# One explicit order for all five engines of a two-layer graph-attention kernel, with operand splits and products issued in two steps

## The chip, the cores and the metric

The kernel runs on one core of a Trainium2 chip. The metric is the device time of one execution in microseconds (us). A statement such as "2055.66 us" is the median of several executions. A ratio is the mean time of one kernel's fast runs over the mean of the other's fast runs in the same rounds, with a 95% interval, so it is not quite the ratio of the medians quoted beside it. A difference under 2% counts as "same".

## The reference, cut to what matters

The input x has 128 batches of 128 tokens by 512 features; adj is one 128x128 matrix used for all batches.

```python
# layer 0: graph convolution, maximum, residual, layer norm
A = einsum('od,bdn->bon', adj, x);  C = A + b
out0 = max(relu(A[:, :, None, :] + (C - A)[:, :, :, None]), axis=-1)
x = layernorm(x + out0)
# layer 1: masked attention with 8 heads, projection, inner norm, residual, layer norm
q, k, v = split(x @ w_qkv)                        # 512 -> 3 * 512
attn = softmax(where(adj == 0, -inf, q @ k.T * scale))
o = (attn @ v) @ w_proj + b_proj
x = layernorm(x + o + (layernorm(o) * gamma + beta))
```

Per batch this is one convolution, eight score and eight attention products with 64 wide heads, and 512-deep products for q, k, v and the projection. The deep products dominate.

## The kernel before

Batches go in 32 groups of four. Precision comes from splitting an operand a into a high part h, a rest l and a third form d, so that one product becomes 12 matmuls of 128x512: four of h, four of l, four of d. In the names of the trace, `x_h x_l x_d` are the split input, `oh ol od` the split attention output (for the last eight batches it lies in the buffers of `w_h w_l w_d`), `po` (as `pp_('o', 48)`) a projection, `pp_(13, 2)` a product of group 13, `psc` scores, `eT` the transposed attention weights, `pa` a convolution, `xb` the residual.

```python
def split(key, src, dsts):
    fh, fl, fd = dsts
    xh = work.tile([P, KC, P], FP, tag="xh", name=f"xh_{key}")
    nc.vector.tensor_scalar(xh.bitcast(I32), src.bitcast(I32), HIGH, None, op0=ALU.bitwise_and)
    hs[key] = fh, xh                               # ScalarE casts xh to fh later: split_high
    nc.vector.tensor_tensor(fl, src, xh, op=ALU.subtract)
    nc.vector.scalar_tensor_tensor(fd, fl.bitcast(FP), -HALF, xh, op0=ALU.mult, op1=ALU.add)

def product(key, two, terms):
    # ... pm, pd: two PSUM banks
    for kc in range(KC):
        h, l, _ = terms(kc)
        nc.tensor.matmul(pm, *h, start=(kc == 0), stop=False)
        nc.tensor.matmul(pm, *l, start=False, stop=(kc == KC - 1))
    for kc in range(KC):
        nc.tensor.matmul(pd, *terms(kc)[2], start=(kc == 0), stop=(kc == KC - 1))
```

The program is written as a plan: each call has a place in us, and the plan is sorted by place. TensorE and ScalarE are pinned to the order of the plan; VectorE, GpSimd and the queue of transfers (SyncE) get their order from a scheduler.

```python
plan.sort(key=lambda p: p[:2])
run([p for p in plan if p[0] < 0], None)
run([p for p in plan if p[0] >= 0], {mybir.EngineType.PE, mybir.EngineType.Activation})
```

Of the kernel before, what the change touches and what calls it, by code (L numbers as in the profile page):

```python
# [10 lines left out]
I32 = mybir.dt.int32  # L11
AF = mybir.ActivationFunctionType
# [12 lines left out]
def tile_adj_resnorm_d2(  # L25
# [37 lines left out]
    nc = tc.nc  # L63
# [19 lines left out]
    xs, x1s, rms, pa, mv0s, pts, hs = {}, {}, {}, {}, {}, {}, {}  # L83
# [101 lines left out]
    def add_0(b):  # L185
        g, i = divmod(b, G)
        if i == 0:
            mv0s[g] = small.tile([P, G, 3], FP, tag="sum0", bufs=2, name=f"sum0_{g}")
        nc.scalar.activation(
            xs[b], xs[b], AF.Identity, bias=rms[g][:, i : i + 1], accum_out=mv0s[g][:, i, 0:1],  # L190
        )
# [35 lines left out]
    def split(key, src, dsts):  # L227

        fh, fl, fd = dsts
        xh = work.tile([P, KC, P], FP, tag="xh", name=f"xh_{key}")  # L230
        nc.vector.tensor_scalar(xh.bitcast(I32), src.bitcast(I32), HIGH, None, op0=ALU.bitwise_and)  # L231
        hs[key] = fh, xh
        nc.vector.tensor_tensor(fl, src, xh, op=ALU.subtract)  # L233
        nc.vector.scalar_tensor_tensor(  # L234
            fd, fl.bitcast(FP), -HALF, xh, op0=ALU.mult, op1=ALU.add,
        )
# [5 lines left out]
    def split_high(key):  # L242
        nc.scalar.copy(*hs.pop(key))


    def product(key, two, terms):
# [7 lines left out]
        for kc in range(KC):  # L254
            h, l, _ = terms(kc)
            nc.tensor.matmul(pm, *h, start=(kc == 0), stop=False)
            nc.tensor.matmul(pm, *l, start=False, stop=(kc == KC - 1))
        for kc in range(KC):
            nc.tensor.matmul(pd, *terms(kc)[2], start=(kc == 0), stop=(kc == KC - 1))
        pps[key] = pm, pd  # L260
# [112 lines left out]
    def project(b):  # L373
        parts = [*zip(oTs.pop(b), proj_forms)]
        product(("o", b), b % 2 == 0, lambda kc: [(f[:, kc, :], w[:, kc, :]) for f, w in parts])
# [59 lines left out]
    plan = []  # L435
# [3 lines left out]


    def weights_step(b, u):
        at(u, transpose_e, b)
        at(u + 1.0, weights_T, b)
        return u + 0.9

    def x_step(b, u):
        at(u, transpose_x, b)
        at(u + 0.5, split_x, b)
        at(u + 3.0, split_high, b)
        return u + 0.45  # L450

    def scores_step(b, u):
        at(u, scores, b)
        at(u + 1.0, masked, b)
        return u + 1.0

    def attend_step(b, u, ready):
        at(u, attend, b)
        at(max(u + 1.0, ready), heads, b)
        at(max(u + 1.0, ready) + 0.8, split_high, ("o", b))  # L460
        return u + 1.0

    def conv_step(b, u):
        at(u, conv, b)
        at(u + 1.0, conv_max, b)
        return u + 0.9

    def dense_step(g, j, u, two):
        at(u, dense, g, j, two)
        at(u + 1.9, dense_main, g, j)  # L470
        at(u + 2.8, dense_rest, g, j)
        return u + 2.8

    def project_step(b, u):
        at(u - 5.0, bias, b)
        at(u, project, b)
        at(u + 1.9, projected_main, b)
        at(u + 2.8, projected_rest, b)
        return u + 2.8

    def normed(b, u, v, w, z):

        at(u - 9.0, residual, b)
        at(u - 3.0, residual_o, b)
        at(u, stats, b, 1)
        at(v, norm_1, b)
        at(w, stats, b, 2)
        at(z, norm_2, b)

    def layer_0(b, u, adds, norms):  # L490

        at(u, relu_0, b, 2)
        for i in range(2):
            at(adds + 0.9 * i, add_0, b + i)
            at(adds + 1.8 + 0.9 * i, stats_0, b + i)
        at(adds + 3.7, rstd_0, b, 2)
        for i in range(2):
            at(norms + 1.5 * i, norm_0, b + i)
            at(norms + 1.0 + 1.5 * i, keep_0, b + i)
            at(norms + 25.0 + 1.5 * i, beta_0, b + i)  # L500

    def first_pair(g, t):

        last, now, nxt = (g - 1) * G, g * G, (g + 1) * G
        u = t
        if g:
            for i in range(2):
                u = weights_step(last + i, u)
        for i in range(2):
            u = x_step(nxt + i, u)  # L510
        for i in range(2):
            at(u + 0.5, load_x, nxt + G + i) if g + 2 < NG else None
        for i in range(2):
            u = scores_step(now + i, u)

        if g:
            for i in range(2):
                u = attend_step(last + i, u, u + 1.0 + 5.3 * i)
        for i in range(2):
            u = dense_step(g, 2 + i, u, i == 1)  # L520
            if g:
                u = project_step(last + i, u)
        return u

    def second_pair(g, t):
        last, now, nxt = (g - 1) * G, g * G, (g + 1) * G
        u = t
        if g:
            for i in range(2, 4):
                u = weights_step(last + i, u)  # L530
        for i in range(2, 4):
            u = x_step(nxt + i, u)
        for i in range(2, 4):
            at(u + 0.5, load_x, nxt + G + i) if g + 2 < NG else None
        for i in range(2, 4):
            u = scores_step(now + i, u)
        if g:
            for i in range(2, 4):
                u = attend_step(last + i, u, u + 1.0 + (0.0, 7.1 if g + 2 < NG else 5.3)[i - 2])
        return u  # L540

    def dense_phase(g, t):

        last, far = (g - 2) * G, (g + 1) * G
        u = t

        def convs(i, u):
            if far < B:
                for k in range(i, i + 2):
                    u = conv_step(far + k, u)  # L550
            return u

        if g:
            u = convs(0, u)
        for n in range(2 * KC):
            if g == 0 and n in (2, 4):
                u = convs(n - 2, u)
            u = dense_step(g, G + n, u, n % 2 == 0 or n == 1 and g > 1)
            if n < 2 and g > 1:
                u = project_step(last + 2 + n, u)  # L560
            if n == 1 and g:
                u = convs(2, u)
        if g < NG - 1:
            for i in range(2):
                u = dense_step(g, i, u, i == 0)
        return u


    for b in range(G):
# [13 lines left out]
        at(u + 8.5 + 0.2 * b, split_high, b)  # L583
        at(u + 9.0, load_x, G + b)
# [6 lines left out]
    layer_0(G, 12.0, 13.0, 19.0)  # L591
    layer_0(G + 2, 19.0, 20.0, 34.0)

    t = dense_phase(0, 0.0)
    for g in range(NG - 1):
        last, far = (g - 1) * G, (g + 2) * G
        u = first_pair(g, t)
        u = second_pair(g, u)
        for i in range(G):
            at(t + (8.7, 13.5, 29.5, 34.0)[i], row_max, g * G + i)  # L600
            at(t + (10.3, 15.5, 30.5, 36.0)[i], exps, g * G + i)
            at(t + (24.0, 30.0, 42.0, 46.0)[i], weights, g * G + i)
        if g:
            normed(last, t + 22.0, t + 31.5, t + 35.5, t + 39.5)
            normed(last + 1, t + 31.0, t + 39.5, t + 43.0, t + 47.0)
            normed(last + 2, t + 45.0, t + 48.5, t + 52.0, t + 56.0)
            normed(last + 3, t + 52.0, t + 56.0, t + 60.0, t + 66.0)
        if far < B:
            for i, places in enumerate(((30.5, 39.5, 53.0), (43.0, 46.0, 66.5)) if g else ((16.0, 17.0, 24.0), (23.0, 24.0, 34.0))):
                layer_0(far + 2 * i, *(t + p for p in places))  # L610
        t = dense_phase(g + 1, u)


    g = NG - 1
    last, now = (g - 1) * G, g * G
    u = t
    def finish_step(b, u):
        at(u - 12.0, residual, b)
        at(u + 4.0, residual_o, b)
        at(u + 5.6, stats, b, 1)  # L620
        at(u + 8.5, norm_1, b)
        at(u + 12.0, stats, b, 2)
        at(u + 16.5, norm_2, b)
        return project_step(b, u)

    def finish_step(b, u):
        at(u - 12.0, residual, b)
        at(u + 4.0, residual_o, b)
        at(u + 5.6, stats, b, 1)
        at(u + 8.5, norm_1, b)  # L630
        at(u + 12.0, stats, b, 2)
        at(u + 16.5, norm_2, b)
        return project_step(b, u)

    for p in (0, 2):
        for i in (p, p + 1):
            u = weights_step(last + i, u)
        for i in (p, p + 1):
            u = scores_step(now + i, u)
        for i in (p, p + 1):  # L640
            u = attend_step(last + i, u, 0.0)
        for i in (p, p + 1):
            u = dense_step(g, i, u, i % 2 == 0)
            u = finish_step(last + i, u)
    for i in range(4):
        v = t + (6.0, 9.0, 22.0, 25.0)[i]
# [48 lines left out]
```

## Time and profile before

The time before is 2055.66 us (median of 3, 2052.22 to 2056.8). I cut the span at the first matmul of three products: (0,6), (2,6) and (31,6). The pieces are the first work, the filling of the pipeline, 29 steady groups, and the tail with its drain.

| before, us | value |
|---|---|
| span start to (0,6) | 34.86 |
| (0,6) to (2,6) | 109.76 |
| (2,6) to (31,6), 29 groups | 1815.70 |
| one undisturbed group | 62.67 |
| (31,6) to the end | 90.45 |

This is the profile of the kernel before by those stretches (the first two rows of the table are one stretch here). The columns are the stretch, its length, then busy us and instructions of TensorE, its weight loads, VectorE, ScalarE and GpSimd, granted clock, share of DMA time, and GB/s.

```profile
0.00:144.62 144.62, 128.86 (x666) 97.07 (x666) 115.04 (x182) 97.53 (x270) 37.80 (x73) 0.94 0.51 123
144.62:1960.32 1815.70, 1798.15 (x10898) 1443.23 (x10897) 1437.49 (x2318) 1295.08 (x3709) 640.31 (x1332) 1.00 0.51 118
1960.32:2050.77 90.45, 72.18 (x473) 59.27 (x471) 67.07 (x117) 56.77 (x154) 34.59 (x79) 0.93 0.33 91
```

### The profile page before, as it was taken

The numbers are of one execution on the slowest core, as the hardware profiler recorded it, in microseconds if no ns is written. First come the engines' busy times: TensorE is split into PE (matmuls) and PEld (weight loads), VectorE is DVE, ScalarE is ACT, GpSimd is POOL, SyncE is SP. The second block draws the span as 40 slices with busy tenths as digits, with TensorE's granted clock in tenths as the row PEclk, the third lists the DMA queues.
The fourth block names the chain that finished last, engine by engine and source line by source line (L and its number), as shares of the span: only waits on it lengthen the run. The fifth ranks groups of instructions, "written<-read, shape, count | busy, mean of one in ns | idle before, by whom it ended". The sixth has DMA issues, their size and how long they took to land.

```text
span 2050.8 us, 35140 instructions
## 1 busy us (share of the span) xinstructions
PE 1999.2 (97%) x12033; PEld 1599.6 (78%) x12033; DVE 1619.6 (79%) x2615; ACT 1449.4 (71%) x4130; POOL 712.7 (35%) x1484
## 2 busy tenths in 40 slices
PE   7999999999999999999999999999999999999996
PEld 4778878778787788787787877887877878778785
DVE  7797777887778877778877788777788777887777
ACT  6776777766777767777667677677776676776766
POOL 3232334333334323333333333233332333332324
PEclk8999999999999999999999999999999999999998
DMA  6445645455544556544555445564445554454623
GB/s 186 98 83 119 139 113 112 107 123 124 129 120 107 108 119 139 120 105 106 123 124 128 120 107 111 119 139 115 106 111 121 125 128 117 108 110 119 140 65 101
DMA packets 134436, 240.67 MB, mean 117 GB/s; under 512 B 14704, under 2 KB 18928, under 8 KB 134256
## 3 DMA queue, kind: packets, MB, share of 16 engines
q1 hardware_dynamic: 97680, 172.27, 26.7%
q0 software_dynamic: 36288, 66.08, 23.4%
q8 instruction: 95, 1.56, 0.3%
q14 instruction: 85, 0.70, 0.1%
q10 hardware_dynamic: 288, 0.07, 0.0%
HBM read 138.74 MB, written 100.66 MB: 117 GB/s over the span
## 4 chain that ended last, share of the span: by engine, by line
PE 82%; DVE 13%; issue 2%; ACT 1%; DMA 1%; POOL 1%; SPq 0%; POOLq 0%; DVEq 0%; ACTq 0%
PE pa L173 6%; PE ppt L339 5%; DVE e L309 4%; PE psc L302 3%; PE pav L352 3%; DVE xh L231 2%; DVE x_l L233 2%; PE ptx L223 2%; DVE x_d L234 2%; DVE ol L233 1%; DMA xb<-o 1%; ACT e L324 0%; DVE nmax L317 0%; POOL sum L409 0%; ACT square L402 0%
## 5 line engine op out<-in xcount | busy, mean ns | idle before, releaser
L324 ACT ACTIVATE e<-e,nmax 128x128 f32<-128x128 f32 x1024 | 396.3, 390 | 10.6 <-DVE nmax L317 10.3
L216 POOL DMA_DIRECT2D x<-in_L_gnn_ln_beta_dram x128 | 112.7, 991 | 443.4 <-DMA x<-xt 439.7
L409 POOL TENSOR_TENSOR sum<-sum,mhalf 128x1 f32<-128x1 f32 (+1 forms) x322 | 204.5, 635 | 26.7
L324 ACT ACTIVATION_READ_ACCUMULATOR e<-e,nmax 128x1 f32 x1024 | 193.5, 189 | 0.0
L391 POOL DMA_DIRECT2D xb<-o x124 | 113.2, 913 | 225.9 <-DVE sums L332 107.3
L402 ACT ACTIVATE square<-o,sum 128x512 bf16<-128x512 f32 x256 | 183.9, 718 | 10.4 <-DVE o L396 8.4
L183 POOL TENSOR_SCALAR rm<-rm,b_sb 128x2 f32<-128x2 f32 (+1 forms) x66 | 66.7, 1011 | 284.8 <-DVE rm L177 259.5
L333 DVE TENSOR_TENSOR e<-e,sums 128x1024 f32<-128x1024 f32 x128 | 154.2, 1223 | 2.2
L317 DVE TENSOR_REDUCE nmax<-e 128x8 f32<-128x1024 f32 x128 | 154.7, 1208 | 0.1
L309 DVE SCALAR_TENSOR_TENSOR e<-psc,mask 128x1024 f32<-128x1024 f32 x128 | 150.4, 1214 | 0.0
L343 ACT COPY eT<-ppt 128x1024 f32<-128x1024 f32 x128 | 123.4, 1015 | 35.0 <-PE ppt L339 35.0
L414 POOL TENSOR_SCALAR sum<-sum 128x1 f32<-128x1 f32 x256 | 99.7, 392 | 122.4 <-DVE o L396 122.2
L396 DVE SCALAR_TENSOR_TENSOR o<-o,sum,xb 128x512 f32<-128x512 f32 x128 | 95.5, 746 | 52.8 <-POOL sum L409 52.8
L408 POOL TENSOR_SCALAR sum<-sum 128x1 f32<-128x1 f32 (+1 forms) x322 | 64.4, 200 | 201.3 <-ACT square L402 186.2
L302 PE MATMUL psc<-qkT 64*128 64x128 f32 x2048 | 131.9, 278 | 0.8 <-ACT eT L343 0.7
L352 PE MATMUL pav<-eT,v 128*64 128x128 f32 x2048 | 127.5, 278 | 2.8 <-ACT eT L343 2.8
L302 PEld LDWEIGHTS psc<-qkT 64*128 64x128 f32 x2048 | 119.4, 188 | 11.9 <-issue 10.4
L173 PE MATMUL pa<-xt,adjT 128*128 128x512 f32 x256 | 126.2, 617 | 0.4 <-DVE adjT L102 0.4
L339 PEld LDWEIGHTS ppt<-ident,e 128*128 128x128 f32 x1024 | 115.7, 141 | 9.5 <-DVE v L291 0.8
L339 PE MATMUL ppt<-ident,e 128*128 128x128 f32 x1024 | 122.4, 272 | 0.6 <-DVE v L291 0.6
L352 PEld LDWEIGHTS pav<-eT,v 128*64 128x64 f32 x2048 | 112.0, 138 | 10.8 <-ACT eT L343 3.3
L423 DVE SCALAR_TENSOR_TENSOR o<-o,sum,gamma_sb 128x512 f32<-128x512 f32 x128 | 95.6, 747 | 31.4 <-ACT square L402 26.6
(4778 smaller groups left out, 5622.1 us busy)
## 6 DMA issues: line engine op xcount, KB each, us to landing
xt<-in_x_dram SPq DMA_DIRECT2D x128, 256.0 KB, 5.1
x<-xt SPq DMA_DIRECT2D x128, 256.0 KB, 3.6
x<-in_L_gnn_ln_beta_dram POOLq DMA_DIRECT2D x128, 256.0 KB, 7.4
xb<-x SPq DMA_DIRECT2D x128, 256.0 KB, 2.7
o<-in_L_gnn_b_proj_dram SPq DMA_DIRECT2D x128, 256.0 KB, 3.5
out_dram<-o SPq DMA_DIRECT2D x128, 256.0 KB, 2.7
xb<-o POOLq DMA_DIRECT2D x124, 256.0 KB, 3.9
wraw<-in_L_gnn_w_qkv_dram SPq DMA_DIRECT2D x12, 256.0 KB, 3.9
```

Source lines behind the costliest of these rows:

```text
L173: nc.tensor.matmul(pa[b], adjT, xs[b], start=True, stop=True)
L302: nc.tensor.matmul(psc[:, s, hp, :], qkT[hs, hp, i, :], qkT[hs, KC + hp, i, :], start=True, stop=True,)
L309: nc.vector.scalar_tensor_tensor(e, pscs.pop(b).rearrange("p s a m -> p (s a) m"), scale, mask_b, op0=ALU.mult, op1=ALU.add,)
L317: nc.vector.tensor_reduce(nmax, es[b], AX.X, ALU.max, negate=True)
L324: nc.scalar.activation(e[:, j, :], e[:, j, :], AF.Exp, bias=nmax[:, j : j + 1], accum_out=sums[:, j : j + 1],)
L333: nc.vector.tensor_tensor(e, e, sums[:, :, None].to_broadcast([P, H, P]), op=ALU.mult)
L339: nc.tensor.transpose(ppts[b][:, j, :], e[:, j, :], ident)
L343: nc.scalar.copy(eTs[b], ppts.pop(b))
L352: nc.tensor.matmul(pavs[b][s * HD : (s + 1) * HD, hp, :], v[:, h * HD : (h + 1) * HD], eT[:, s * HP + hp, :], start=True, stop=True,)
L391: nc.gpsimd.dma_start(xbs[b], os[b], accum_op=ALU.add)
L402: nc.scalar.activation(square, x, AF.Square, bias=s[:, 0:1], scale=-float(D), accum_out=s[:, 1:2],)
L409: nc.gpsimd.tensor_tensor(s, s, mhalf[:, :n], op=ALU.pow)
```

## The change

The intent is to take away the stalls that an automatic VectorE order leaves. Every engine is pinned, and each VectorE, ScalarE, GpSimd and transfer call gets a place relative to the TensorE step that it serves. The third split step (`split_d`) and the third part of a product (`product_d`) become calls of their own, so other work can stand between. TensorE's steps also get a new order: transposes of weights (T) and of inputs (x) take turns, product 5 goes ahead of product 4 and product 8 ahead of 7. Which products write to which PSUM pool changes too (`two`).

```diff
-        hs[key] = fh, xh
+        hs[key] = dsts, xh
         nc.vector.tensor_tensor(fl, src, xh, op=ALU.subtract)
+    def split_d(key):
+        (_, fl, fd), xh = hs[key]
         nc.vector.scalar_tensor_tensor(fd, fl.bitcast(FP), -HALF, xh, op0=ALU.mult, op1=ALU.add)
 ... the same for product and product_d ...
+    O = {... 'pair_order': [('T', 0), ('x', 1), ('T', 1), ('x', 0), ('S', 0), ('S', 1), ('AV', 0), ('AV', 1),
+                            ('dense', 2), ('po', 0), ('dense', 3), ('po', 1), ...],
+         'po_rest': [0.0, 0.48, 0.0, -0.81], 'x_hl': [0.9, 1.26, 0.32, 0.33], ...}
+        elif kind == "AV":
+            at(u, attend, b)
+            free = pe["po", b - 1] + 0.1 if b % 2 and b < B - 2 * G else -9.0
+            p = pe["po", b]
+            at(min(max(u + O["o_hl"][i], free), p - 0.2), heads, b)
+            at(min(max(u + O["o_high"][i], free + 0.01), p - 0.1), split_high, ("o", b))
+            at(min(max(u + O["o_d"][i], free + 1.85), p + 1.8), split_d, ("o", b))
 ... places for all other calls; the old step functions go ...
-    run([...], {mybir.EngineType.PE, mybir.EngineType.Activation})
+    run([...], {E.PE, E.Activation, E.DVE, E.Pool, E.SP})
```

## The prediction

> **What bounds the kernel now.** I read the page first, then the busy time by stretches, then the instructions of one group in order of time, engine by engine.
>
> ```profile
> span 2050.8 us, 35140 instructions
> PE 1999.2 (97%) x12033; PEld 1599.6 (78%) x12033; DVE 1619.6 (79%) x2615; ACT 1449.4 (71%) x4130; POOL 712.7 (35%) x1484
> PE 82%; DVE 13%; issue 2%; ACT 1%; DMA 1%; POOL 1%; SPq 0%; POOLq 0%; DVEq 0%; ACTq 0%
> ```
>
> TensorE is the bound, but its 97% says little about how much is left: the chain of work that ended last leaves it for VectorE for 13% of the span. The kernel handles 128 batches in 32 groups of 4, so I cut the middle of the run at the first matmul of the product (g,6) of successive groups:
>
> ```profile
> 833.99:896.66 62.67, 62.09 (x379) 49.83 (x377) 49.59 (x81) 44.83 (x130) 22.11 (x46) 1.00 0.52 119
> 896.66:959.32 62.66, 62.09 (x378) 49.81 (x377) 49.57 (x81) 44.81 (x130) 22.32 (x47) 1.00 0.50 119
> ```
>
> The columns are length, then busy us of PE, PEld, DVE, ACT and POOL, clock, DMA share, GB/s. A group takes 62.67 us, the same every time, at full clock; DMA is at half. The 0.58 us of idle PE per group understates what is lost, because a matmul's record overlaps the next one's. Starts tell more:
>
> ```profile
> 863.37 0.50 PE L256 MATMUL pm_(13, 2)_8666<-w_h,x_h 128*128 128x512 f32 x1
> ...
> 865.33 1.10 PE L259 MATMUL pd_(13, 2)_8667<-w_d,x_d 128*128 128x512 f32 x4
> 866.41 0.49 PE L256 MATMUL pp_('o', 48)_8687<-p_h,oh 128*128 128x512 f32 x1
> 867.48 0.50 PE L257 MATMUL pp_('o', 48)_8687<-p_l,ol 128*128 128x512 f32 x1 [0.58 <-DVE ol L233]
> 867.82 0.40 PE L256 MATMUL pp_('o', 48)_8687<-p_h,oh 128*128 128x512 f32 x1
> ...
> 870.15 0.40 PE L256 MATMUL pp_(13, 3)_8721<-w_h,x_h 128*128 128x512 f32 x1
> ```
>
> Undisturbed, matmuls start 0.233 us apart, so a product of 12 takes 2.80 us. This projection takes 870.15 - 866.41 = 3.74, so it loses **0.94**; its first matmul came another 0.14 late (four matmuls to 866.41 take 1.08, not 0.93), waiting for oh. That is 1.08 us a group, once a group. What holds it is in the VectorE rows of the same moment:
>
> ```profile
> 862.76 2.35 DVE L309 SCALAR_TENSOR_TENSOR e<-psc,mask 128x1024 f32<-128x1024 f32 x2
> 865.02 0.68 DVE L231 TENSOR_SCALAR xh_('o', 48)_8649<-pav 128x512 int32<-128x512 int32 x1
> 865.62 1.21 DVE L317 TENSOR_REDUCE nmax<-e 128x8 f32<-128x1024 f32 x1
> 866.75 0.68 DVE L233 TENSOR_TENSOR ol<-pav,xh_('o', 48)_8649 128x512 fp32r<-128x512 f32 x1
> ```
>
> A row maximum nobody needs yet stands between the two halves of the operand split, and both masks stand ahead of it. The last kind of loss is at the end:
>
> ```profile
> 2005.60 0.50 PE L257 MATMUL pp_('o', 122)_20237<-p_l,w_l 128*128 128x512 f32 x1 [1.29 <-DVE w_l L233]
> ...
> 2018.06 3.48 PE L352 MATMUL pav<-eT,v 128*64 128x128 f32 x32 [2.41 <-ACT eT L343]
> ...
> 2032.56 0.49 PE L256 MATMUL pp_('o', 126)_20497<-p_h,w_h 128*128 128x512 f32 x1 [1.18 <-ACT w_h L243]
> ```
>
> **What the Trainium skill says.** "Perfetto Trace Analysis", Identifying the Most-Contended Engine: matmul busy time is a bad measure of nearness to the roofline, as pipelined matmuls mislead. The trace agrees: 97% busy, yet 1.08 us per group recoverable. "TensorE: Matmul & The Clock Gate", Part 2, Step-by-step: matmuls stay in program order and only weight loads are pulled ahead. That fits the 0.94 us: nothing passed the waiting matmul. The same page, Architectural detail: ScalarE and VectorE are strict FIFO. The VectorE rows fit: ol runs behind nmax although its input had been there. "Perfetto Trace Analysis", Optimizing Tensor Performance: independent matmul groups should rotate through PSUM banks; the change alters that rotation.
>
> **The change, part by part.** No work is added or removed. The built programs have the same 5251, 2361 and 1702 rows on TensorE, VectorE and ScalarE; only order and PSUM banks differ.
>
> *Floor of a group.* 16 products x 2.80 = 44.80. From the starts in the TensorE rows: two pairs each of weight transposes (1.75), x transposes (0.97), scores (1.99), attention (1.90) and convolutions (3.51 for the two) give 13.22 + 3.51 = 16.73, and the step from attention to a product 0.10. Sum 61.63, rounding included; directly, 62.67 - 1.08 = **61.59**. I use the latter.
>
> *First half of the group.* New order: T0 x1 T1 x0 S0 S1 AV0 AV1 d2 po0. VectorE's is xh, xl of x1; xh, xl of x0; mask0; xd0, xd1; xh, ol of o0; mask1; od0; nmax0. With T0 at 0 and start-to-start durations from its rows of before (split steps 0.60, mask 1.17, row maximum 1.13): x0's input is there at 2.8, xl0 is done at 4.0, mask0 at 5.2, xd0 and xd1 at 6.3, ol at 7.5. The projection is due at 9.3. It has 1.8 us in hand where it was 1.1 late, so the stall goes: **-1.08 a group**, in the 30 groups that have it: 30 x 1.08 = 32.4 us.
>
> *Second half.* I carried the same sum on: ol of o2 done 0.9 before po2 is due, ol of o3 0.75 before po3; a convolution maximum frees the bank of product 5's second part 0.8 early. On ScalarE (a row's eight exponentials 3.1, eT copy 1.0), exponentials 1 end near 18.3, a square near 19.0, the two eT copies at 20.0 and 21.1; scores 2 and 3, which need those banks, are due at 20.4 and 21.3. That leaves only 0.1 to 0.3: the tightest place. I allow 0.1 us a group: **+3**.
>
> *Start.* Before product (0,4) starts at 25.03 us nearly the same scheduler is at work; later the first groups lose about 2.5 to first-time waits. Product (0,5) now goes first and VectorE is pinned to the weight splits. I take -1, with 3 either way.
>
> *End.* From the first transpose of the tail at 1977.12 to the last projection's end near 2038.5 there are 61.4 us; the steps sum to 8 x 0.87 + 4 x 0.99 + 8 x 0.95 + 12 x 2.80 = 52.1, so 9 are stalls. The transposes for the last batches get their weights sooner now, but a transpose still waits for its copy (0.4 to 0.6) and a projection for its split (0.6) with little between: about 4 remain. **-5**. The drain after the last matmul (about 12) keeps its chain.
>
> Sum: -32.4 + 3 - 1 - 5 = -35.4, so 2055.7 - 35.4 = **2020 us**.
>
> **The rivals.**
> 1. *A new wait in each group.* All queues are pinned, so one instruction waiting at VectorE's head delays all behind it. For: the 0.1 to 0.3 us at scores 2 and 3, and GpSimd, whose scalar statistics now stand behind DMA issues of 0.9 to 1.0 us. Against: VectorE works 50 of 62.7 us, and its slack lies in the second part of the products. At 0.5 us a group: 2032.
> 2. *VectorE's automatic order was worth something.* Its old scheduler filled gaps; a pinned order cannot. If VectorE falls behind by a microsecond at both attention pairs, the stall comes back in another place: about 2050. A wait worse than today's would need over 1 us a group: 2060 or more.
> 3. *The places remove more than I found.* With no residual stall, and a clean start and tail: 2055.7 - 32.4 - 4 - 7 = 2012. The transposes and convolutions have their own floor, so hardly below 2008.
>
> The transfers are no rival: half the DMA time is free, and loads are a group ahead.
>
> **Range and chances.** The steady part is regular to 0.02 us, so any error there counts 30 times; the plan looks tuned for just these waits, which speaks for the low half. The range 2009 to 2036 spans rival 3 to somewhat beyond rival 1. Two per cent faster means below about 2015, just under my estimate: 0.34. Slower by 2% needs rival 2 at its worst: 0.02. Within 2%: 0.64.
>
> **What would show it.** Right: groups of 61.6 to 61.8 us in the middle; no wait of the first projection on ol; product starts 2.80 apart; unchanged busy time on every engine; stalls in the tail halved. Wrong: groups above 62.0 with a wait on eT copies before scores (rival 1) or on ol, oh or a freed PSUM bank (rival 2); a first product much after 25 us; or groups below 61.4, which would mean my floor holds a hidden wait.

## The result and the profile after

The changed kernel takes 2039.85 us (2038.49 to 2040.23, 4 runs) beside 2054.43 us for the kernel before (2052.22 to 2056.8, 4 runs): ratio 0.9928, interval 0.991 to 0.9945. It is 14.6 us faster where 35.4 us were predicted, and the time is 3.85 us above the top of the predicted range. All outputs are right.

The line of busy times on the page, then the same three stretches, both of the kernel after:

```profile
PE 1995.0 (98%) x12033; PEld 1601.2 (79%) x12033; DVE 1652.2 (81%) x2615; ACT 1455.4 (71%) x4130; POOL 694.2 (34%) x1484
```

```profile
0.00:147.50 147.50, 128.69 (x665) 97.92 (x666) 116.08 (x181) 97.80 (x270) 31.83 (x70) 0.93 0.49 117
147.50:1941.84 1794.34, 1791.75 (x10898) 1444.18 (x10897) 1465.76 (x2316) 1300.65 (x3708) 626.33 (x1333) 1.00 0.52 119
1941.84:2038.45 96.61, 74.58 (x473) 59.09 (x471) 70.37 (x119) 56.98 (x156) 36.07 (x84) 0.92 0.37 99
```

The middle gained 21.36 us, but the start lost 2.88 and the tail 6.16. Two small signs matter later: VectorE's busy time rose by 32.6 us with the same 2615 instructions, and the tail's mean clock is 0.92 beside 0.93.

**The middle.** One group of the kernel after, in the same columns (the next one takes 61.86):

```profile
828.09:889.95 61.87, 61.87 (x378) 49.86 (x377) 50.60 (x81) 44.91 (x129) 21.51 (x47) 1.00 0.54 120
```

A group gained 0.80 us, from 62.67 to 61.87. The stall that the prediction named is gone. These are TensorE's instructions in order of time (start, us, engine, line, what), first around the first projection of a group, then around the fourth:

```profile
921.29 1.10 PE L269 MATMUL pd_(14, 2)_9368<-w_d,x_d 128*128 128x512 f32 x4
922.22 0.40 PE L261 MATMUL pm_('o', 52)_9397<-p_h,oh 128*128 128x512 f32 x1
922.46 0.40 PE L262 MATMUL pm_('o', 52)_9397<-p_l,ol 128*128 128x512 f32 x1
...
944.62 0.40 PE L261 MATMUL pp_(15, 4)_9658<-x_h,w_h 128*128 128x512 f32 x1
...
947.60 0.50 PE L261 MATMUL pm_('o', 55)_9679<-p_h,oh 128*128 128x512 f32 x1
947.94 0.39 PE L262 MATMUL pm_('o', 55)_9679<-p_l,ol 128*128 128x512 f32 x1
...
950.50 1.88 PE L174 MATMUL pa<-xt,adjT 128*128 128x512 f32 x4
```

Projection 52 starts 0.93 us after the last block of four, which is those four matmuls at 0.233, and its second matmul comes 0.24 later: no wait. But the product (15,4) takes 947.60 - 944.62 = 2.98 us and projection 55 takes 950.50 - 947.60 = 2.90 instead of 2.80 each. That is a new loss of 0.18 + 0.10 = 0.28 us a group, at the **fourth** projection, where none was before (the kernel before starts product (14,5) at 889.75, projection 51 at 892.54 and the convolution after it at 895.34). The list of waits for this window is empty; only the starts show it. VectorE at the same moment, kernel after:

```profile
942.81 0.68 DVE L178 TENSOR_REDUCE rm<-pa 128x1 f32<-128x512 f32 x1
943.41 0.68 DVE L391 SCALAR_TENSOR_TENSOR o<-pp_('o', 54)_9593,o 128x512 f32<-128x512 f32 x1
944.01 0.74 DVE L432 SCALAR_TENSOR_TENSOR o<-o,sum,gamma_sb 128x512 f32<-128x512 f32 x1
944.86 0.75 DVE L405 SCALAR_TENSOR_TENSOR o<-o,sum,xb 128x512 f32<-128x512 f32 x1
...
945.54 0.69 DVE L405 SCALAR_TENSOR_TENSOR o<-pp_('o', 54)_9593,o 128x512 f32<-128x512 f32 x1
...
946.15 0.69 DVE L232 TENSOR_SCALAR xh_('o', 55)_9642<-pav 128x512 int32<-128x512 int32 x1
946.87 0.69 DVE L234 TENSOR_TENSOR ol<-pav,xh_('o', 55)_9642 128x512 fp32r<-128x512 f32 x1
```

Here six steps from 942.81 to 946.87 take 4.06 us; at 0.60 each they would take 3.60. Independent neighbours start 0.60 apart, although each record lasts 0.68. A step that reads what its neighbour wrote starts later: xh to ol 0.72, the two norm lines 0.85. The excess of 0.46 us is larger than the loss of 0.28. Over the whole second half of the group, from xh of its first input (932.13) to this ol, the excess over 0.60 at such neighbours is 0.13 + 0.11 + 0.11 + 0.13 + 0.25 + 0.08 + 0.12 = 0.93 us.

The first matmul of projection 55 reads oh, ScalarE's cast of xh. Its row:

```profile
946.93 0.62 ACT L248 CAST oh<-xh_('o', 55)_9642 128x512 fp32r<-128x512 f32 x1 [0.32 <-DVE xh_('o', 55)_9642 L232]
```

ScalarE had been idle for 0.32 us, waiting for VectorE's xh, and the cast ends at 947.55, 0.05 us before the projection starts. So ScalarE passes the delay on; it doesn't make it.

**The tail.** TensorE, then VectorE, then the stretch that begins with projection 123 (its clock is the third number from the end), all of the kernel after:

```profile
1996.88 0.80 PE L261 MATMUL pm_('o', 123)_20460<-p_h,w_h 128*128 128x512 f32 x1 [4.49 <-ACT w_h L248]
1997.47 0.63 PE L262 MATMUL pm_('o', 123)_20460<-p_l,w_l 128*128 128x512 f32 x1
```

```profile
1980.73 0.75 DVE L432 SCALAR_TENSOR_TENSOR o<-o,sum,gamma_sb 128x512 f32<-128x512 f32 x1 [2.95 <-DMA xb<-o]
...
1994.34 0.69 DVE L232 TENSOR_SCALAR xh_('o', 123)_20439<-pav 128x512 int32<-128x512 int32 x1
```

```profile
1996.80:2001.50 4.70, 4.62 (x11) 3.66 (x12) 2.83 (x5) 1.22 (x4) 1.65 (x2) 0.50 0.72 183
```

Projection 123 waits 4.49 us for its split, which VectorE begins only at 1994.34. VectorE stood idle for 2.95 us at a norm (the row at 1980.73), which waits for the transfer that adds o to the residual. Then it works for 13.6 us, without a wait in its rows, on the norms, masks and weights that its order puts ahead of the split. So the late residual can account for at most 2.95 of the 4.49 us; the order accounts for the rest. The wait costs twice: afterwards matmuls start some 0.43 us apart instead of 0.233 at a granted clock of 0.50, where the stretch before the wait has 1.00. The Trainium skill, "TensorE: Matmul & The Clock Gate", Part 1, says that an idle window of about 3.4 us halves TensorE's clock; this trace agrees, with 0.50 right after 4.49 us of waiting. Other runs told of below don't fit that length: in e12 the clock is 0.50 in the 2.4 us after a wait of 2.52, and in e15 it stays 1.00 after one of 2.85.

**The start.** The stretch to (0,6) is unchanged (34.86 and 34.89 us); from (0,6) to (2,6) it grew from 109.76 to 112.61. Two parts are netted in this: (0,6) to (1,6) grew from 46.31 to 50.74, while (1,6) to (2,6), a group with the old stall, shrank from 63.45 to 61.87. The waits of the transfers' queue in the kernel after between 50 and 80 us (total, times, longest), and then its transfers between 50 and 85 us (count, size, median us from issue to landing):

```profile
SPq L90 <- DMA x<-xt: 12.2, 3, 7.1
```

```profile
x<-in_L_gnn_ln_beta_dram POOLq DMA_DIRECT2D x6, 256.0 KB, 8.3
x<-xt SPq DMA_DIRECT2D x4, 256.0 KB, 7.1
xt<-in_x_dram SPq DMA_DIRECT2D x4, 256.0 KB, 6.4
```

Loads of x (L90) wait 12.2 us in all for the stores `x<-xt` that free their buffers, and these stores take 7.1 us (median) to land. In the same stretch GpSimd issues the accumulating transfers of beta for the first group, four in one burst:

```profile
56.28 3.61 POOL L217 DMA_DIRECT2D x<-in_L_gnn_ln_beta_dram  x4
```

In the kernel before, these four go out one at a time, at 16.54, 20.36, 28.00 and 30.24 us.

### The profile page after: what moved, and what is told of

Its sections match the earlier page's. It is cut to its first block, busy times and chain, and to the rows that moved or that the text cites. A ratio compares the mean times of both kernels' runs of the same rounds, so it can differ in the third digit from the quotient of the medians.

```text
span 2038.5 us, 35386 instructions
## 1 busy us (share of the span) xinstructions
PE 1995.0 (98%) x12033; PEld 1601.2 (79%) x12033; DVE 1652.2 (81%) x2615; ACT 1455.4 (71%) x4130; POOL 694.2 (34%) x1484
## 5 line engine op out<-in xcount | busy, mean ns | idle before, releaser
L400 POOL DMA_DIRECT2D xb<-o x124 | 132.8, 1071 | 479.2 <-DVE o L405 449.3
L423 POOL TENSOR_SCALAR sum<-sum 128x1 f32<-128x1 f32 x256 | 89.7, 350 | 281.4 <-DVE o L405 280.8
L318 DVE SCALAR_TENSOR_TENSOR e<-psc,mask 128x1024 f32<-128x1024 f32 x128 | 155.5, 1216 | 2.3 <-PE psc L311 2.3
L217 POOL DMA_DIRECT2D x<-in_L_gnn_ln_beta_dram x128 | 140.3, 1196 | 10.3 <-issue 10.3
L348 PE MATMUL ppt<-ident,e 128*128 128x128 f32 x1024 | 132.3, 273 | 0.5 <-DVE qkT L300 0.5
L190 ACT ACTIVATE xt<-xt,rm 128x512 f32<-128x512 f32 x128 | 91.4, 715 | 37.7 <-POOL rm L184 37.7
L440 ACT ACTIVATE o<-o,sum 128x512 f32<-128x512 f32 x128 | 103.0, 806 | 16.5 <-POOL sum L426 16.5
```

The lines of the kernel that those rows point to most:

```text
L217: nc.gpsimd.dma_start(x1s[b], row(ln_beta), accum_op=ALU.add)
L318: nc.vector.scalar_tensor_tensor(e, pscs.pop(b).rearrange("p s a m -> p (s a) m"), scale, mask_b, op0=ALU.mult, op1=ALU.add,)
L348: nc.tensor.transpose(ppts[b][:, j, :], e[:, j, :], ident)
L400: nc.gpsimd.dma_start(xbs[b], os[b], accum_op=ALU.add)
```

## The experiments

The kernel before was run beside each set; its medians were 2052.46, 2056.22, 2052.44 and 2051.65 us in the four sets. "After" is the changed kernel; it wasn't run again in these sets, which ran on different chips, so a difference between absolute times of different sets is good to a few us only (the medians of the kernel before themselves differ by 4.6), and the ratios are the safer guide. Stretches are those of the one profiled run: of after and e16 it was the slowest of the four, of e13 and e14 the fastest.

### Which pinned engine does what

**e1_only_two_pinned** pins only TensorE and ScalarE, as before, with everything else of the change kept.

```diff
-    run([...], {E.PE, E.Activation, E.DVE, E.Pool, E.SP})
+    run([...], {E.PE, E.Activation})
```

> The changed kernel with only TensorE and ScalarE in the explicit order, as before; VectorE, GpSimd and the DMA queue are left to the automatic order again. The built order shows both row maxima (nmax) back between xh and ol of the first projection of a group. Theory A (the middle of the run was won by VectorE's explicit order, which finishes the operand split first; start and tail were lost by the explicit orders): the wait on ol returns, a group takes 62.5 to 62.8 us instead of 61.87, the tail shortens by some 5 us; total 2045 to 2058. Rival B (the gain is from TensorE's new order, the products in two steps and the new PSUM banks): a group stays at 61.6 to 61.9 and the total falls to 2025 to 2035.

It took 2277.27 us, ratio 1.1088 (1.1054 to 1.1123). In 200 us of its middle the list of TensorE's waits begins

```profile
PE pa L174 <- DVE x_l L234: 10.5, 3, 3.8
```

so convolutions wait up to 3.8 us for a PSUM bank that VectorE's input split holds (both kinds of tile come from one pool of four). With the new TensorE order and new places, the scheduler's order of VectorE is far worse than it was for the old plan. Neither forecast had this size. Why its choice is so bad I did not settle; what follows is that the gain of the change cannot be had from the TensorE order alone.

**e6_before_vector_pinned** is the counterpart: the kernel before with VectorE pinned by the old places.

```diff
-    run([...], {mybir.EngineType.PE, mybir.EngineType.Activation})
+    run([...], {mybir.EngineType.PE, mybir.EngineType.Activation, mybir.EngineType.DVE})
```

> The kernel before with one thing changed: VectorE also in the explicit order, by the places it already had. The built order has xh, ol, od of the first projection ahead of the row maximum. Theory A: the wait on ol (0.94 us a group) goes, a group takes 61.6 to 62.0 us and the total falls to 2022 to 2036, without any of the new places. Rival B (the new order on TensorE and the split in two steps are needed, because three split steps ahead of the masks hold VectorE up): a wait returns elsewhere, a group takes 62.4 us or more, total 2045 to 2060.

It took 2190.52 us, ratio 1.067 (1.0654 to 1.0686). In the middle it has a wait that neither kernel had:

```profile
PE pm_('o', 43)_7693 L256 <- ACT oh L243: 2.6, 1, 2.6
```

It comes once a group; groups took about 65.84 us, and neither forecast came near. So pinning by itself is worth nothing; the old places were never meant to be VectorE's order. The gain of the change needs new places and the pinning together.

**e2_dma_automatic** leaves GpSimd and the transfers' queue to the scheduler and pins the other three.

```diff
-    run([...], {E.PE, E.Activation, E.DVE, E.Pool, E.SP})
+    run([...], {E.PE, E.Activation, E.DVE})
```

> The changed kernel with GpSimd and the DMA queue automatic; TensorE, ScalarE and VectorE stay explicit. Theory A: the middle stays at 61.8 to 61.9 us a group, as nothing there waited long for GpSimd or a DMA. Of the losses at the start (+2.9 us) and in the tail (+6.2 us), the part that comes from late loads goes: if the queue's order is their cause, total 2030 to 2034; if VectorE's places in the tail are the cause, total 2037 to 2042. Rival C (the explicit queue also costs in the middle): a group falls below 61.7.

It took 2033.66 us, ratio 0.9909 (0.9894 to 0.9923). The groups stayed at 61.87, the tail went from 96.61 to 95.53, and (0,6) to (2,6) from 112.61 to 105.22. The last of these is what pinning GpSimd and the transfers lost at the start. In the tail VectorE's wait for the residual falls from 2.95 to 1.00 us, and that of projection 123 from 4.49 to 2.52. The tail takes 94.90 to 95.53 with the transfers' queue automatic (e2, e11, e12) and 96.61 to 97.91 with it pinned and the same places there (after, e7, e16), so pinning costs some 2 us there too. Only VectorE's pinning differs between e1 and this run: 2277.27 against 2033.66 us.

### The new loss at the fourth projection

**e3_norm_later** moves a norm of VectorE behind the split of the fourth projection.

```diff
-                    'norm_1': [19.0, 21.67, 15.07, 18.26],
+                    'norm_1': [21.5, 21.67, 15.07, 18.26],
```

> The changed kernel with one place moved: the first batch's norm_1 goes from 19.0 to 21.5 after its projection, that is behind the operand split of the group's fourth projection instead of ahead of it. Theory A (0.28 us a group is lost at that fourth projection because VectorE is 0.8 us later than the sum of its durations, dependent pairs being 0.72 apart and not 0.60): the split comes about 1.5 us earlier, the loss goes, a group takes 61.6 us and the total falls by 7 to 9 us, to about 2031. Rival (ScalarE, not VectorE, makes the operand late, or the wait only moves to another step): the group stays at 61.8 or more and the total within 3 us of the changed kernel.

It took 2082.84 us, ratio 1.0145 (1.013 to 1.016). Product (15,4) and projection 55 were back at 2.80, so the norm did stand in the way, but the cure was worse; neither forecast had that. VectorE's waits in 200 us of its middle:

```profile
DVE o L432 <- DMA xb<-o: 11.1, 3, 3.9
```

The norm is what frees the residual's buffer. Later norm, later load into that buffer, later accumulation, and VectorE's head then waits 3.5 to 3.9 us in each group for it. Behind it two q and k products, (14,6) and (14,7) in one group, take 0.87 and 0.96 us longer by their starts; the list of waits has 0.4 to 0.8 at each such product, for banks. A strict order makes one late transfer everybody's wait.

**e7_rest_later** moves another instruction instead, which frees nothing that is short: the last part of the third projection goes behind xh and ol of the fourth.

```diff
-            at(u + 2.8 + O["po_rest"][i], projected_rest, b)
+            at(u + 2.8 + (1.75 if i == 2 and b < B - 2 * G else O["po_rest"][i]), projected_rest, b)
```

> The changed kernel with one place moved in the middle: the addition of the second product of the third projection of a group (projected_rest) goes 1.75 later, to between ol and od of the fourth projection's operand split. Nothing that frees a residual buffer moves, other than in the earlier attempt, where the loss at the fourth projection went but a late residual held VectorE and two new waits of 0.9 us came. Theory A: the split comes 0.6 us earlier, the 0.28 us go and nothing takes their place: 61.6 us a group, total 7 to 9 us under the changed kernel, near 2032. Rival (ScalarE's exponentials, or a residual that is late in any case, set the end): 61.8 us or more a group.

It took 2032.12 us, ratio 0.9885 (0.987 to 0.99), 7.7 us under the kernel after. One of its groups:

```profile
885.63:947.24 61.61, 61.61 (x379) 49.93 (x377) 50.54 (x81) 45.13 (x129) 21.90 (x47) 1.00 0.51 120
```

A group took 0.26 us less, product (15,4) and projection 55 take 2.80 again, and 61.6 is the floor of 61.59 that the prediction computed. In the steady part VectorE's order differs from that of after in this one instruction alone. The cause of the 0.28 is thereby shown: the split came one VectorE instruction too late.

### What the two-step splits and the transposes' turns are worth

**e8_one_step** puts the third split step directly behind the second again.

```diff
-            at(u + O["x_d"][i], split_d, b)
+            at(u + O["x_hl"][i], split_d, b)
...
-            at(min(max(u + O["o_d"][i], free + 1.85), p + 1.8), split_d, ("o", b))
+            at(min(max(u + O["o_hl"][i], free), p - 0.2), split_d, ("o", b))
```

> The changed kernel with the operand split in one step again: its third instruction (d) directly behind the second (l), for x and for the attention output. My count by VectorE's order: for x the third instructions stood ahead of the first attention split anyway, only one mask moves behind them, and in the second half they stood directly behind already. If the split in two steps matters little: 61.8 to 62.2 us a group, total 2037 to 2050. Rival (the split in two steps is what lets the projections start in time): the first projection of a group waits again, 62.5 us or more a group, total 2060 or more.

It took 2056.49 us, ratio 1.0003 (0.9988 to 1.0018), so the whole gain is gone. Groups took 62.41, between the two forecasts. In 200 us of its middle TensorE's waits are

```profile
PE psc L311 <- ACT eT L352: 1.9, 3, 0.6
```

so once a group the scores wait 0.65 us for the PSUM bank that a copy of attention weights still holds; the step from the second x transpose to the scores takes 1.25 us instead of 0.53. The two-step split is thus worth 62.41 - 61.87 = 0.54 us a group, but through the scores, not through the projection (the scores lose 0.72, and product (15,4) gets 0.18 back).

**e10_TTxx** transposes both weights first and then both inputs.

```diff
-         'pair_order': [('T', 0), ('x', 1), ('T', 1), ('x', 0), ... ('T', 2), ('x', 3), ('T', 3), ('x', 2),
+         'pair_order': [('T', 0), ('T', 1), ('x', 1), ('x', 0), ... ('T', 2), ('T', 3), ('x', 3), ('x', 2),
```

> The changed kernel with TensorE's old order at the head of each pair: both weight transposes, then both x transposes, in place of taking turns; all else by the same places. The first x arrives on VectorE 0.87 us later. Theory A (in the second half of a group VectorE has no slack up to the fourth projection, so whatever starts it later is paid in full): 62.5 to 63.0 us a group, total 2058 to 2075. Rival (VectorE has slack there, the turns do nothing): 61.9 us a group, total within 5 us of the changed kernel.

It took 2090.64 us, ratio 1.017 (1.0155 to 1.0185), with groups of 63.56: projections started late and scores waited 0.33. The places of other calls go with their steps, so VectorE's order changes a little too: one x_d moves behind a split and a mask. With that change included, letting the transposes take turns is worth some 1.7 us a group.

Not tested alone are product 5 ahead of 4, product 8 ahead of 7, and the new use of the PSUM pools, to which the prediction applies the Trainium skill. The call `product_d` of its own changes nothing on TensorE: in both traces the third part directly follows the first two in every product.

### The start

**e11_rest_and_dma** joins e7 and e2.

> The changed kernel with the two edits that helped, together: the third projection's second part 1.75 us later in VectorE's order, and the transfers' queue and GpSimd left to the scheduler. If the two losses are apart (start in the transfers' order, 0.25 us a group in VectorE's), the gains add: 7.7 us from the first (2039.85 to 2032.12) and about 6 from the second (2039.85 to 2033.66), so some 2026 us, groups of 61.6, first product (2,6) at 143. Rival: the automatic queue answers to VectorE's order, and later residual work makes it late; then the groups stay above 61.8 and the time is 2031 or more.

It took 2026.00 us (2024.01 to 2029.4), ratio 0.9868 (0.9853 to 0.9883). Groups of 61.61, and (0,6) to (2,6) in 104.98: the gains add. This beats both kernels.

**e12_sp_automatic** leaves only the transfers' queue (SyncE) to the scheduler.

```diff
-    run([...], {E.PE, E.Activation, E.DVE, E.Pool, E.SP})
+    run([...], {E.PE, E.Activation, E.DVE, E.Pool})
```

> The changed kernel with only the transfers' queue (SyncE) left to the scheduler, GpSimd still pinned. If the loads of x, late in the pinned queue, cost the start, product (2,6) starts at 143 and the time is near 2034, as with both automatic. Rival: GpSimd's pinned order costs it (its small scalar operations stand behind its DMA issues and hold the norms); then (2,6) stays at 147 and the time at 2039 to 2040.

It took 2038.00 us, ratio 0.9923 (0.9907 to 0.994), with (2,6) at 148.46 and (0,6) to (2,6) in 113.43. My theory, the loads' own order, fell; the rival, GpSimd's order, stood for the start, though I had named the wrong instructions in it. In the tail it was the queue: VectorE's wait for the residual was 1.04 us here, that of projection 123 2.52, much as in e2. The trace pointed to the burst of beta transfers at 56 us.

**e16_beta_early** moves these four alone, with all engines pinned.

```diff
-        at(30.0 + b, beta_0, b)
+        at(1.0 + b, beta_0, b)
```

> The changed kernel with the four beta accumulates of the first group 29 us earlier in GpSimd's order, all engines still pinned. If their burst at 56 us is what slows the stores, and so the loads of x, product (2,6) starts at about 143 instead of 147.5 and the time is about 2035.5. Rival: they wait for the first group's stores there and hold GpSimd's small operations behind them, or the queue of transfers is the other half of the cause; then (2,6) is at 146 or later and the time above 2038.

The transfers of this kernel between 50 and 85 us, in the form shown for the kernel after:

```profile
x<-xt SPq DMA_DIRECT2D x4, 256.0 KB, 2.0
xt<-in_x_dram SPq DMA_DIRECT2D x4, 256.0 KB, 2.9
```

The stores land in 2.0 instead of 7.1 us, the loads in 2.9 instead of 6.4, and (0,6) to (2,6) shrinks from 112.61 to 106.77. The loads' waits for these stores fall from 12.2 to 2.3 us in all. That is the mechanism, shown by moving the burst away. A second pair agrees: e17 below differs from e7 at the start in this edit alone, and has 104.99 where e7 has 110.75. The total moved less: 2036.31 us (2032.53 to 2040.04), ratio 0.9916 (0.9899 to 0.9932), and (2,6) came at 145.97 beside 147.50, close to the rival's 146. In its profiled run (0,6) itself came at 39.21 us instead of 34.89. In the profiled runs of e2, e11 and e13 to e17, which have these transfers early by this edit or by the scheduler, (0,6) came between 35.94 and 39.43; in the kernels with GpSimd pinned and these transfers late it came between 34.59 and 35.79. That they compete with the first loads of weights would fit this, but it was not tested, and early transfers alone don't do it: the kernel before and e6 have them early too and reach (0,6) at 34.86 and 33.22. The cause stays open.

### The tail

**e4_tail_splits** gives the splits of the last eight batches places right behind their attention, and a norm a later place, all engines pinned.

```diff
+            if b >= B - 2 * G:
+                at(u + 1.0, heads, b)
+                at(u + 1.8, split_high, ("o", b))
+                at(u + 2.94, split_d, ("o", b))
+                continue
...
-                   'norm_1': [7.89, 8.5, 7.45, 9.78],      # 'final'
+                   'norm_1': [10.0, 8.5, 7.45, 9.78],
```

> The changed kernel with places moved in the tail alone: for the last eight batches the operand split (high, low, rest) follows directly after the attention product of its own batch, instead of up to just ahead of its projection, and one norm_1 of the last four goes behind the last splits. Theory A (the tail lost its time because VectorE in its explicit order reaches these splits late: projections 123, 125, 126 and 127 waited 4.5, 1.1, 0.5 and 2.0 us for their operand): the tail from the first matmul of product (31,6) to the end shortens from 96.6 us by 5 to 9 us, total 2031 to 2035, the middle unchanged at 61.87 us a group. Rival (the late loads of the pinned DMA queue hold the tail, whatever VectorE's places): the tail shortens by less than 3 us.

It took 2044.05 us, ratio 0.9939 (0.9922 to 0.9955); the tail grew from 96.61 to 100.52. Projection 123 was on time, but VectorE then stood 3.44 us at a norm for its residual, and an attention product waited 5.34 us for copied weights. The wait had moved.

**e13_tail_and_dma** repeats it with e11's edits (the transfers automatic).

> The kernel of this job's first run plus the earlier places of the operand splits in the tail that lost 3.9 us there when all queues were pinned. If they lost because the pinned queue's loads came late (VectorE's head waiting for residuals), then with the automatic queue the tail from product (31,6) to the end gets shorter than 95.5 us by about 3, and the time is about 2023. Rival: they lost because ScalarE's copies and the late parts stand in a bad order; then the tail is 98 or more and the time is 2028 to 2031.

It took 2027.07 us, ratio 0.9871 (0.9856 to 0.9885), tail 95.32. Neither theory met this: the automatic queue took back the loss of e4 (100.52), yet the earlier splits were worth nothing beside e11 (94.90), since an attention product still waited 4.6 us for copied weights.

**e14_one_tail_split** is e11 ("this job's first run") with earlier places for batch 123 alone.

```diff
+            if b == B - G - 1:
+                at(u + 1.0, heads, b)
+                at(u + 1.8, split_high, ("o", b))
+                at(u + 2.94, split_d, ("o", b))
+                continue
```

> The kernel of this job's first run with the earlier places for one batch alone, 123, whose projection waited 2.52 us for its operand with the automatic queue. If the wait is worth its length, the time is 2.5 us under the first run of this job, some 2023.5 us. Rival: something behind it (the mask, the row maximum, a norm) is pushed back and the wait moves to a transpose or to the next projection; then the time stays within 1 us of the first run.

It took 2025.95 us, ratio 0.9866 (0.9851 to 0.9881), the same as e11: the rival. The 2.52 us at projection 123 became 4.6 us at an attention product. ScalarE's rows show why: its copy of those weights stood behind a square of batch 123 that waited 3.94 us for VectorE.

**e15_two_more_places** is e14 and moves that square behind the copy, and a norm behind what the square waits for.

```diff
-                  'norm_1': [8.13, 9.06, 7.55, 8.5],        # 'last'
+                  'norm_1': [8.13, 9.06, 7.75, 8.5],
...
-                  'stats_1': [3.76, 4.99, 4.38, 4.65],      # 'last'
+                  'stats_1': [3.76, 4.99, 4.38, 4.95],
```

> e14 with two places in the tail moved: the first statistics of batch 123 behind the copy of batch 125's weights on ScalarE, and the norm of batch 122 behind the last part of batch 123 on VectorE. In e14 that copy stood 3.94 us behind a square that waited for VectorE. If that is the cause, the attention product of batch 125 starts about 4 us earlier and the time falls by 3 to 4 us, to about 2022. Rival: the split of batch 124 or 125, or the end of the drain, takes the wait over; then the time stays within 1 us of e14's 2026.

It took 2023.46 us (2020.32 to 2026.7), ratio 0.9859 (0.9845 to 0.9874). The tail of the profiled run fell from 96.30 to 92.78, by the 3 to 4 us expected, but the ratio moved only from e14's 0.9866 to 0.9859, with intervals that overlap, so a gain in the whole time isn't shown. The waits for copied weights fell from 5.4 us in all to 0.8. Part went on as a wait of 2.8 at projection 124. It is the fastest version run, though its interval overlaps that of e11.

**e17_all_pinned** has the edits of e15 (e7's among them) and e16, and all five engines pinned.

> All places of e15 and e16 and the later third part, with all five engines pinned as in the change. If only places were wrong, it equals e15 within 2 us (about 2022 to 2025). If a pinned order of the transfers loses by itself (the head of a queue waits and all behind it wait), the tail stays several us longer and the time is 2028 or more.

It took 2028.56 us (2024.22 to 2031.66), ratio 0.9883 (0.9867 to 0.9898). Its start (36.39 and 104.99) and middle (1786.88) match those of e15 (37.80, 104.98, 1785.99) but for the start's scatter; its tail is 97.57 against 92.78. VectorE's waits for residuals in the tail, first of e15, then of e17:

```profile
DVE o L432 <- DMA xb<-o: 1.0, 1, 1.0
```

```profile
DVE o L432 <- DMA xb<-o: 3.8, 2, 3.2
```

So in the tail, the pinned order of GpSimd and the transfers costs some 5 us with the places of this plan, through residuals that come late to VectorE. Better places for them may exist; I tried none.

The stretches side by side:

| kernel | to (0,6) | (0,6) to (2,6) | (2,6) to (31,6) | tail | median us |
|---|---|---|---|---|---|
| before | 34.86 | 109.76 | 1815.70 | 90.45 | 2054.43 |
| after | 34.89 | 112.61 | 1794.34 | 96.61 | 2039.85 |
| e2 | 37.80 | 105.22 | 1793.76 | 95.53 | 2033.66 |
| e7 | 35.13 | 110.75 | 1788.00 | 97.66 | 2032.12 |
| e11 | 39.43 | 104.98 | 1786.01 | 94.90 | 2026.00 |
| e15 | 37.80 | 104.98 | 1785.99 | 92.78 | 2023.46 |
| e17 | 36.39 | 104.99 | 1786.88 | 97.57 | 2028.56 |

One profiled run stands behind each row, so the stretch to (0,6) scatters by up to 3.5 us and the tail by 1.3 between kernels that are alike there. The middle agrees to a few tenths.

## Why the prediction was right or wrong

The step that failed most is the one called *End*; *Start* and *Second half* failed too. The account of the first half held.

**What bounds the kernel, and the first half of the group: right.** The named stall of the first projection is gone, its product takes 2.80, and the list of waits has no entry for it. The 1.08 us came in full (0.80 gained a group plus the 0.28 newly lost). The sum was close: ol ends 7.9 us after the first transpose (7.5 predicted) and 1.6 us before the projection starts (1.8 predicted). The floor of 61.59 us was right too: most groups of e7 and e11 take 61.58 to 61.62. The counts of program rows that the prediction quotes are in no run's record; the profiles count the same TensorE, VectorE and ScalarE instructions before and after (12033, 2615, 4130).

**Second half: wrong in place and size.** The step said that ol of the fourth projection would be done 0.75 us before it is due, and that scores 2 and 3 were the tightest place, 0.1 us a group. (Its own figures leave 0.4 and 0.2 us there, not "0.1 to 0.3".) The scores lost nothing; the fourth projection lost 0.28. The term that was mis-sized is VectorE's split step of 0.60: this distance, read where other instructions stood between, is 0.72 where a step follows the one it reads from, and 0.85 for the norm pair. The old automatic order had such instructions between, and the pinned order does not. ol ended at 947.56 where the projection was due at 947.42, so it came 0.75 + 0.14 = 0.89 us later than predicted; the excess of 0.93 us counted over the half covers that. This is a sum over rows; no run varied the distance alone. VectorE's busy time, predicted unchanged, rose by 32.6 us, which fits records that no longer overlap. Per undisturbed group the gain was 0.80 instead of 0.98 us. The measured middle has a further 0.06 a group less (21.36 / 29 = 0.74), because two groups took longer (62.86 and 62.15), and the last, at 60.83 already before, gained only 0.17.

**Start: -1 predicted, +2.9 measured,** just outside the 3 us given either way of -1. The step looked only at first products and VectorE. It missed that pinning GpSimd gathers four accumulating transfers into a burst beside the stores on which the next loads wait (e12, e16). The prediction's 30th group, with its gain, lies in this stretch, so the start proper, (0,6) to (1,6), did worse still: +4.43 us.

**End: -5 predicted, +6.2 measured: the largest error,** 11.2 us. (The profiled pair differs by 2050.77 - 2038.45 = 12.3 us, so the sum of -35.4 missed by 23.1: 11.2 here, 3.9 at the start, 8.0 in the middle.) The step said that transposes get their weights sooner and about 4 us of stalls remain. It counted the stalls of the old order and did not walk VectorE's new order there. It took as given that a residual would be there when its norm comes up. The pinned order puts norms, masks and weights ahead of the splits, and a late residual then holds everything behind it (2.95 us); together they make a wait of 4.49 us on TensorE with a slow clock after it. With the queue automatic (e11) the tail is still 94.90 us against 90.45 before, and e15's places take 2.1 us of that; the rest stays open. The prediction wrote "the transfers are no rival: half the DMA time is free". Bandwidth was free, but latency in a fixed order was not: e2, e16 and e17 all gain or lose by transfers.

**The rivals.** Rival 1, a new wait in each group, came true at about half its size and at another place. Rival 2, that the automatic order was worth something, came true twice: for VectorE as 0.28 us a group, and for GpSimd and the transfers as about 6 us by the medians, 4 by the ratios (e2). Its other side is that the automatic order is worth nothing with the new plan (e1). Rival 3, a clean start and tail, didn't come: even the further edits of e15 stop at 2023.46.

**Range and chances.** The class "within 2%" was the likelier one, at 0.64, and came. The range failed because start and tail were taken as small terms with good signs; both had the other sign.

## What to carry to other kernels

Pin an engine only where its order decides something, and give new places with it: here VectorE pinned with the new places carried the gain, while GpSimd and the transfers were better left automatic, because a fixed queue turns one late transfer into a wait for all behind it. In a pinned order, count dependent neighbours at their own distance and put an independent instruction between them. After the steady state is checked, walk the start and the tail instruction by instruction; they gave back 9 of the 21 us gained, and a wait removed there moved on three times (e4, e13, e14) before one edit shortened the tail of its profiled run.

## What the Trainium skill lacked or had wrong

- "TensorE: Matmul & The Clock Gate", Part 1, puts the slow clock after an idle window of about 3.4 us. Here it was 0.50 right after a wait of 2.52 us (e12) and 1.00 after one of 2.85 (e15).
- "VectorE: DVE Perf Modes", The DRAIN you can't avoid, says for eight copies in a row that a semaphore after each costs nothing extra, and that an instruction that isn't held starts before the pipe is empty. It lacks how far apart two instructions start when the second reads what the first wrote. Here independent 128x512 neighbours start 0.60 apart while each record lasts 0.68, a neighbour that reads the result starts after 0.72, and the norm pair after 0.85.
- No page gives how long plain stores take beside a burst of accumulating transfers: with four of them in one burst, stores of 256 KB took 7.1 us to land (after), and 2.0 us without (e16).
- No page warns that, because TensorE's records overlap (0.39 to 0.50 us long, 0.233 apart), a short wait leaves no idle time between them: 0.18 and 0.10 us in every group were to be seen only as start-to-start times of 2.98 and 2.90 instead of 2.80.
